# One of 25 products per chunk on another engine, and a new order of loads, in a deformable convolution

## The chip, the cores and the metric

The kernel runs on one core of a Trainium2 chip. The metric is the time on the device in microseconds (us), the median of several runs. A core has five engines with a queue of instructions each: TensorE (PE), VectorE (DVE), ScalarE (ACT), GpSimd (POOL) and SyncE (SP), which here only issues transfers. They run side by side and wait for each other through semaphores. SBUF is the memory on the core, PSUM the banks into which PE accumulates, HBM the memory outside.

## The reference

Four layers follow each other on x of shape (8, 128, 96, 96), each of the form x + f(groupnorm(x)). Layers 1 to 3 (a 3x3 convolution, a depthwise one with signs, a recurrence over rows) are not touched. The change lies in layer 0, a deformable convolution. Cut to what matters:

```python
x1 = gelu(layernorm(depthwise3x3(x)))            # per image
om = x1 @ om_w.T + om_b                          # per pixel and group: 9 offsets (x, y), 9 masks
loc = pixel + tap + offset
samp = bilinear(x, loc)                          # zero outside the image
out = sum over 9 taps of samp * mask
x = x + out
```

There are 8 groups of 16 channels. While every offset is below 1, a bilinear sample is a sum over the 5 x 5 neighbours of a pixel, each with a weight that does not depend on the channel within the group. The kernel uses this: out is the sum of 25 products "weights times shifted rows".

## The kernel before, in words

Layer 0 takes the 8 images one after the other. An image has 12 groups of rows for its depthwise convolution (`NST`), and then 6 **chunks** (`BR`), each made of 16 rows that stand 6 apart; chunk n is chunk n % 6 of image n // 6, 48 in all. The same stage runs for different chunks at the same time:

- **Image** (`image`, once per image, a whole image ahead): SP loads the rows of x into `xq` (L492), DVE takes statistics (L590), ACT normalizes in place (L666), SP writes the normalized rows to HBM as `xnd` (L679, 24 copies per image), PE does the depthwise convolution, nine taps for each group of rows, into the one PSUM bank pair `ps_w` (L720). ACT evicts it to one of two `x1` buffers (L751), SP stores it as `x1d` (L766). In image 0 some groups of rows (`FIRST_ON_DVE`) are convolved on DVE (L710, L712), stored by L770, and the other groups take turns between `ps_w` and `ps_s`.
- **Projection** (`chunk`, some two chunks ahead): SP loads the chunk's rows as `x1c` (L843), ACT applies gelu (L847), PE multiplies by the projection's weights in four pieces, each through `ps_w` (L862), ACT evicts them to `oe` (L870), of which there are two buffers, two pieces in each. SP stores each `oe` to HBM (`omd`, L878) and loads all back in another layout as `om` (L885; one buffer).
- **Tents and weights** (about one chunk ahead): ACT makes from the offsets the three tents `ty` and `tx` per axis (L900 to L909; four buffers of each). POOL multiplies and adds them into the 25 weights per tap position, in three shifts that each begin with L935 (the third one frees `om`), then L941, L950, L958, L960, and two sums L969 into `wx` (two buffers). For chunk 0 two of the three shifts are on DVE.
- **Products**: for each of five vertical shifts, ACT copies the weights into a PSUM bank `ps_wb` (two of them, L1011), and DVE makes five products `pr` = weights x rows (L1023; three `pr` buffers). The rows are in one of five **row slots** `xs` (L827), which hold the chunk's 16 rows at one vertical offset; chunk dy of an image uses slots dy to dy + 4. PE adds each product into `ps_s` through identity matrices (L988: 16 matmuls, which the trace shows as 32 records), after a first addition of the normalized input itself. There is one `ps_s`; ACT evicts it at the chunk's end to `y` (L1055), SP stores `y` (L1072).

In the last chunk seven of the 25 products (`LAST_ON_POOL`) are made by POOL (L1031), straight from `wx`, into an `oe` buffer, since no projection is left that needs it.

The order of every engine's queue is fixed when the program is written out. A planner (`Plan`) gets tasks with an engine, a cost, dependences and a due time; it plays them through and writes each engine's instructions in the order in which it would start them. Due times are multiples of the chunk's length with offsets: `LOAD_AT`, `NORM_AT`, `COPY_AT`, `CONV_AT` for the image's steps, `X1_AT` and `OM_STEP` for the projection, `SLOT_AT` for the row slots, `CONV_BEHIND` for the convolution on PE from image 1 on. Pools marked in order give their buffers in the order in which they were asked for. On the chip the semaphores follow the data only, so a dependence in the planner between tasks that share no data sets nothing but their order.

```python
shared = n == N * BR - 1 and k in LAST_ON_POOL
pr = plan.buf("oe" if shared else "pr")
...
if shared:
    t = plan.task("POOL", 3.65, mul_pool, [*known[sy], slot.load], when - POOL_W, uses=[wx, pr, slot], lag=0.1)
else:
    t = plan.task("DVE", 1.72, mul, [cp, slot.load], when, uses=[wb, pr, slot], lag=0.1)
```

Of the kernel before, what the change touches and what calls it, by code (L numbers as in the profile page):

```python
# [19 lines left out]
P = 128  # L20
# [4 lines left out]
RS = 2  # L25
# [26 lines left out]
    return sorted(every, key=lambda s: (s[0] % NR, s[1] % NR))  # L52


FIRST_ON_DVE = (2, 5, 8, 11)
CH, SHIFT, PE_KEEP = 47.0, 8.6, 4.0
LOAD_AT, NORM_AT, COPY_AT, COPY_LATE, COPY_FROM = -140, -90, -70, 220, 52
CONV_AT, CONV_STEP, CONV_PACE, CONV_GAP = -60, 20, 0.9, 0.0
X1_AT, OM_STEP, SLOT_AT = -95, 2.7, 25
BEHIND, AHEAD, CONV_BEHIND = 40, 60, 40  # L60
HOLD, BEHIND1 = False, 40
LAST_ON_POOL, EACH_ON_POOL, POOL_W = (4, 7, 10, 13, 16, 19, 22), (16,), 20


class Buf:
# [12 lines left out]
class Plan:  # L78
# [20 lines left out]
    def task(self, engine, cost, fn, deps, prio, uses=(), lag=0.05, shape=None, gap=0.0, first=-1e9, move=0.0):  # L99
        t = SimpleNamespace(engine=engine, cost=cost, fn=fn, prio=prio, uses=list(uses), lag=lag, after=[], shape=shape, gap=gap, first=first, move=move)  # L100
        t.number, t.wait = len(self.tasks), len(deps)
        for d in deps:
            d.after.append(t)
        for b in t.uses:
            b.left += 1
        self.tasks.append(t)
        return t
# [94 lines left out]
def kernel(  # L202
# [25 lines left out]
    N, _, H, W = x.shape  # L228
# [7 lines left out]
    NB, HC = 2, P // 2  # L236
    YB, BR = 16, H // 16
# [184 lines left out]
    with ExitStack() as ph:  # L422
# [47 lines left out]
        for name, n, shape, psum, in_order in (  # L470
            ("s", 1, [P, NQ, 512], True, True), ("wb", 2, [P, 512], True, True), ("w", 1, [P, CB, 512], True, False),
            ("xs", 5, [P, GC, XW], False, True), ("pr", 3, [P, GC, W], False, True), ("y", 1, [P, NQ, FB], False, True),
            ("om", 1, [P, 3, K2, W], False, True), ("ty", 4, [P, K2, W], False, True), ("tx", 4, [P, K2, W], False, True),
            ("wx", 2, [P, 3, 3, NS, W], False, True), ("x1", 2, [P, NB, FB], False, False),
            ("x1c", 1, [P, YB, W], False, True), ("oe", 2, [P, YB, W], False, True), 
        ):
            pool = pp if psum else wp
            tiles = [pool.tile(shape, F32, name=f"{'ps_' if psum else ''}{name}{k}") for k in range(n)]
            plan.pool(name, tiles, in_order=in_order)
            if name == "y":  # L480
                spare = tiles[0][:].rearrange("p q f -> p (q f)")[:, : 6 * W].rearrange("p (k w) -> p k w", w=W)
            if name == "wx":
                bias_in, bias_by_g = (tiles[1][0:1, 0, j].rearrange("p s w -> p (s w)")[:, : 3 * GK] for j in range(2))
                put_off(bias_in, om_b.rearrange("k r -> (k r)").unsqueeze(0))

        def load_rows(i, lo, hi, on=nc.sync, js=range(NB)):

            for b in range(NB):
                a, z = (max(lo, RP), hi) if b == 0 else (lo, min(hi, XR - RP))
                top = b * HB - RP  # L490
                for j in js:
                    on.dma_start(xq[half(b), a:z, j, RS : RS + W], x[i, half(j), top + a : top + z, :])  # L492
# [2 lines left out]

            return ap.rearrange("p (b f) -> p b f", b=NB)[:, :, c * FB : (c + 1) * FB]

        free_rows = {}
        smalls = []
        for i in range(2):  # L500
            smalls.append({
# [64 lines left out]
        def image(i, at, before=()):  # L566
# [4 lines left out]
            loads = []  # L571
            step = 1 if i else 2
            for m in range(0, NST, step):
                rows = (0 if m == 0 else RP + m * RB, RP + (m + step) * RB if m < NST - step else XR)
                deps = [t for k in range(m - 1, m + step + 1) for t in free_rows.get((i - 1, k), [])] + list(before)
                when = at + LOAD_AT + 3 * m
                if i:
                    loads += [[task("SP", 2.7, lambda r=rows: load_rows(i, *r), deps, when, lag=0.6, move=1.7)]]
                    continue
                loads += [[  # L580
                    plan.task(e, 2.1, lambda r=rows, on=on, j=j: load_rows(0, *r, on, [j]), [], -1e7 + m, lag=0.6, move=1.7)
                    for j, (e, on) in enumerate((("SP", nc.sync), ("ACT", nc.scalar)))
                ]] * step
            st = small["st"][:].rearrange("p (j m k) -> p j m k", j=NB, k=6)
            stats = []
            for m in range(NST):
                for j in range(NB):
                    stats.append(task(
                        "DVE", 0.55,
                        lambda m=m, j=j: nc.vector.bn_stats(  # L590
                            st[:, j, m, :], xq[:, RP + m * RB : RP + (m + 1) * RB, j, RS : RS + W]
                        ),
                        loads[m][j : j + 1] if i == 0 else loads[m], at + LOAD_AT + 8 + 3 * m,
                    ))
            mv, mean, d, sd, sc, bi = (small[k] for k in ("mv", "mean", "d", "sd", "sc", "bi"))
            mv2 = mv[:].rearrange("p (j k) -> p j k", k=2)
# [16 lines left out]
            def end(ps):  # L613
# [3 lines left out]
            t = plan.task("DVE", 0.9, aggr, stats, -1e6)  # L617
            b1 = plan.buf("w")
            t = plan.task(
                "PE", 0.7, lambda: means(b1.tile), [t, *ready], -1e6, uses=[b1], lag=0.1,  # L620
            )
# [70 lines left out]
            for c in range(NST):  # L692
# [3 lines left out]
                prev = []  # L696
# [32 lines left out]
                for t in range(K2):  # L729
                    if on_dve:  # L730
                        prev = [plan.task(
                            "DVE", 0.92, lambda t=t, tap=tap_dve: [tap(t, j) for j in range(NB)], need + prev,
                            when + CONV_PACE * t, uses=[ps], lag=0.05,
                        )]
                    else:
                        prev = [task(
                            "PE", 0.8, lambda t=t, tap=tap: tap(t), need + prev,
                            when + CONV_PACE * t + (CONV_BEHIND - BEHIND if i else 0), uses=[ps], lag=0.5, shape=32,
                            gap=CONV_GAP if i == 1 else 0.0,
                        )]  # L740
# [78 lines left out]
            slots = {}  # L819
# [15 lines left out]
        def chunk(i, dy, made):  # L835
# [53 lines left out]
                kept, at + X1_AT + 25, uses=[om], lag=0.6, move=4.6,  # L889
            )]  # L890

            wx = plan.buf("wx")
            cols = lambda ap: ap.rearrange("p k w -> p (k w)")
            tent = {}
# [110 lines left out]
            k = 0  # L1005
            for sy in range(NS):
                wb = plan.buf("wb")
                d, y = places[sy]
                cp = plan.task(
                    "ACT", 0.62,  # L1010
                    lambda wb=wb, d=d, y=y: nc.scalar.activation(  # L1011
                        wb.tile[:, : NS * W], wx.tile[:, d, y].rearrange("p x w -> p (x w)"), AF.Identity
                    ),
                    known[sy], at + SHIFT * (sy - 1) - AHEAD, uses=[wb, wx], lag=0.1,
                )
                slot = slots[dy + sy]
                for sx in range(NS):
                    shared = n == N * BR - 1 and k in LAST_ON_POOL
                    pr = plan.buf("oe" if shared else "pr")
                    when = at + SHIFT * sy + SHIFT / NS * sx  # L1020

                    def mul(wb=wb, pr=pr, slot=slot, sx=sx):
                        nc.vector.tensor_tensor(  # L1023
                            pr.tile[:],
                            wb.tile[:, sx * W : (sx + 1) * W].unsqueeze(1).to_broadcast([P, GC, W]),
                            slot.tile[:, :, sx : sx + W],
                            ALU.mult,
                        )

                    def mul_pool(pr=pr, slot=slot, sx=sx, d=d, y=y):  # L1030
                        nc.gpsimd.tensor_tensor(  # L1031
                            pr.tile[:],
                            wx.tile[:, d, y, sx].unsqueeze(1).to_broadcast([P, GC, W]),
                            slot.tile[:, :, sx : sx + W],
                            ALU.mult,
# [6 lines that stand above are left out]
                    k += 1  # L1042
                    adds.append(plan.task(
                        "PE", 0.82,
                        lambda pr=pr, last=(k == NS * NS): add_all(
                            lambda rows32, f: idr[rows32, :],
                            lambda rows32, f: pr.tile[rows32, 4 * f : 4 * f + 4, :],
                            False, last,
                        ),
                        [t, adds[-1]], when + 2, uses=[pr, total], lag=0.5, shape=32,  # L1050
                    ))
# [992 lines left out]
```

## Time and profile before

| | |
|---|---|
| median of 3 runs | 4487.97 us (4481.05 to 4493.4) |
| the profiled execution's own time | 4487.25 us |
| its span, from the first to the last instruction | 4485.5 us |
| of it layer 0 (to the last chunk's end) | about 2440 us |
| mean granted TensorE clock | 0.965 |
| busy over the span: PE, DVE, ACT, POOL | 91%, 87%, 56%, 70% |

A page row of groups reads: line, engine, operation, output <- inputs by the program's names, shapes, count | busy us, mean ns of one | idle time of the engine just before these instructions, and what ended it. A row of waits reads: who waited <- for whom: us in total, times, longest. A row of the stretches reads: stretch, its length, busy us of each engine with the count of its instructions, granted clock, share of the DMA engines, GB/s. A row of the timeline reads: start, length, engine, line, operation, tiles, count. PEld is the weight load of PE.

### The profile page before, as it was taken

The numbers are of one execution on the slowest core, as the hardware profiler recorded it, in microseconds if no ns is written. First come the engines' busy times: TensorE is split into PE (matmuls) and PEld (weight loads), VectorE is DVE, ScalarE is ACT, GpSimd is POOL, SyncE is SP. The second block draws the span as 40 slices with busy tenths as digits, with TensorE's granted clock in tenths as the row PEclk, the third lists the DMA queues.
The fourth block names the chain that finished last, engine by engine and source line by source line (L and its number), as shares of the span: only waits on it lengthen the run. The fifth ranks groups of instructions, "written<-read, shape, count | busy, mean of one in ns | idle before, by whom it ended". The sixth has DMA issues, their size and how long they took to land. (4 is left out here: it accounts for less than half of the span.)

```text
span 4485.5 us, 168975 instructions
## 1 busy us (share of the span) xinstructions
PE 4066.2 (91%) x75910; PEld 2594.3 (58%) x75910; DVE 3915.5 (87%) x4828; ACT 2510.9 (56%) x3579; POOL 3127.5 (70%) x2191
## 2 busy tenths in 40 slices
PE   4598998989989989899866999999999979999999
PEld 2254564545545546455322555555555548999999
DVE  5599999999999999988897589999999967888887
ACT  3545647456475565654542377777887773333332
POOL 0288787877978878788797599999999961222222
PEclk9799999999999999999898999999999989999999
DMA  7765756648566585573632222233222223232231
GB/s 150 192 169 148 207 147 181 183 136 218 146 174 187 138 220 143 158 187 114 178 93 66 62 68 69 72 78 75 69 73 72 63 59 100 88 110 99 99 113 71
DMA packets 756925, 558.03 MB, mean 124 GB/s; under 512 B 616706, under 2 KB 739219, under 8 KB 750051
## 3 DMA queue, kind: packets, MB, share of 16 engines
q1 hardware_dynamic: 723458, 505.33, 41.9%
q10 hardware_dynamic: 32368, 40.25, 2.7%
q8 instruction: 598, 9.80, 0.9%
q0 software_dynamic: 368, 1.57, 0.1%
q14 instruction: 133, 1.08, 0.1%
HBM read 291.39 MB, written 255.66 MB: 122 GB/s over the span
## 5 line engine op out<-in xcount | busy, mean ns | idle before, releaser
L1023 DVE TENSOR_TENSOR pr<-ps_wb,xs 128x1536 f32<-128x1536 f32 x1193 | 2006.4, 1749 | 126.1 <-PE ps_s L988 94.1
L988 PE MATMUL ps_s<-pr,idr 32*32 32x384 f32 x38176 | 1500.9, 507 | 157.5 <-DVE pr L1023 117.6
L988 PEld LDWEIGHTS ps_s<-pr,idr 32*32 32x32 f32 x38176 | 688.3, 104 | 641.9 <-DVE pr L1023 334.2
L720 PE MATMUL ps_w<-xq,dwd 32*32 32x384 f32 x12672 | 901.4, 497 | 33.3 <-issue 23.2
L1520 PE MATMUL pv_C<-dC,km 128*128 128x384 f32 x2304 | 779.6, 492 | 22.8 <-DVE vn L1537 9.7
L1520 PEld LDWEIGHTS pv_C<-dC,km 128*128 128x128 f32 x2304 | 425.7, 190 | 373.4 <-issue 53.4
L1894 POOL TENSOR_TENSOR xtD<-xtD,cr 128x384 f32<-128x384 f32 x192 | 192.5, 1003 | 597.8 <-ACT cr L1893 535.7
L935 POOL TENSOR_TENSOR ty<-ty,om 128x864 f32<-128x864 f32 x142 | 289.3, 2037 | 438.1 <-ACT ty L908 244.4
L1659 DVE SCALAR_TENSOR_TENSOR pd_C<-xqC,w2s,pd_C 128x768 f32<-128x768 f32 x546 | 554.6, 1016 | 41.3 <-ACT pd_C L1687 33.9
L720 PEld LDWEIGHTS ps_w<-xq,dwd 32*32 32x32 f32 x12672 | 400.5, 104 | 217.1 <-issue 115.3
L960 POOL TENSOR_TENSOR wx<-wx,tmp 128x576 f32<-128x576 f32 x284 | 402.8, 1418 | 22.3
L1955 PE MATMUL ps_b<-tr,km 128*128 128x192 f32 x2304 | 407.0, 325 | 0.7 <-DVE tr L1940 0.7
L1955 PE MATMUL ps_a<-tr,km 128*128 128x192 f32 x2304 | 405.4, 324 | 0.0
L958 POOL TENSOR_TENSOR tmp<-tx,ty 128x576 f32<-128x576 f32 x284 | 403.8, 1422 | 0.0
L1676 POOL TENSOR_TENSOR ptC<-ptC,ptC 128x768 f32<-128x768 f32 x222 | 403.0, 1832 | 0.8
L1507 POOL TENSOR_TENSOR dC<-ywC 128x392 f32<-128x392 f32 x384 | 357.3, 958 | 62.6 <-PE pv_C L1520 29.0
L941 POOL TENSOR_TENSOR wx<-tx,ty 128x864 f32<-128x864 f32 x142 | 289.9, 2042 | 145.8 <-ACT tx L907 128.2
L1955 PEld LDWEIGHTS ps_b<-tr,km 128*128 128x128 f32 x2304 | 380.9, 189 | 0.7 <-ACT sd_oC L1795 0.7
L1955 PEld LDWEIGHTS ps_a<-tr,km 128*128 128x128 f32 x2304 | 379.3, 188 | 0.0
L862 PE MATMUL ps_w<-x1c,omg 128*108 128x384 f32 x768 | 321.9, 545 | 47.1 <-ACT x1c L847 24.2
L1011 ACT ACTIVATE ps_wb<-wx 128x480 f32<-128x480 f32 x240 | 136.5, 569 | 407.3 <-DVE pr L1023 367.3
L1667 ACT ACTIVATE ptC<-vn,wsg 128x768 f32<-128x768 f32 x318 | 286.8, 927 | 105.7 <-POOL ptC L1676 53.9
(240 smaller groups left out, 5740.0 us busy)
## 6 DMA issues: line engine op xcount, KB each, us to landing
xs<-xnd SPq DMA_DIRECT2D x80, 800.0 KB
omd<-oe SPq DMA_DIRECT2D x96, 648.0 KB
om<-omd SPq DMA_DIRECT2D x48, 1296.0 KB
xnd<-xq SPq DMA_DIRECT2D x192, 200.0 KB
x1c<-x1d SPq DMA_DIRECT2D x48, 768.0 KB
y<-y SPq DMA_DIRECT2D x192, 192.0 KB
x<-oC SPq DMA_DIRECT2D x192, 192.0 KB
out<-xtD ACTq DMA_DIRECT2D x24, 1536.0 KB
```

Source lines behind the costliest of these rows:

```text
L720: nc.tensor.matmul(ps.tile[to : to + 32, b, :FB], dwd[of : of + 32, j, t, :], xq[of : of + 32, r0 : r0 + RB, j, c0 : c0 + W], start=(t == ...
L862: nc.tensor.matmul(ps.tile[:HM, b, :FB], omg[:, m * HM : (m + 1) * HM], rows[:, f0 : f0 + FB], start=True, stop=True)
L941: lambda on, s: on.tensor_tensor(flat(wx.tile[:, v, :, 1 : NS - 1]), flat(grid(tx)), flat(grid(ty)), ALU.mult),
L958: on.tensor_tensor(part, flat(grid(te)[:, :, ks : ks + 2]), flat(grid(ty)[:, :, ks : ks + 2]), ALU.mult)
L960: on.tensor_tensor(to, to, part, ALU.add)
L988: nc.tensor.matmul(total.tile[32 * f : 32 * f + 32, r, :FB], weights(rows32, f), of(rows32, f), start=first, stop=last)
L1023: nc.vector.tensor_tensor(pr.tile[:], wb.tile[:, sx * W : (sx + 1) * W].unsqueeze(1).to_broadcast([P, GC, W]), slot.tile[:, :, sx : sx + W ...
L1507: lambda k=k, a=a, b=b, op=op: nc.gpsimd.tensor_tensor(d.tile[:, k], yw.tile[:, a : a + CR - 1 : 2, :], yw.tile[:, b : b + CR - 1 : 2, :], op,
L1520: nc.tensor.matmul(flat(ps), km1[:, k, x_, :], d.tile[:, k, :, x_ : x_ + W], start=(x_ == 0), stop=(x_ == 2))
L1659: nc.vector.scalar_tensor_tensor(view, rows8(src, t, h), w[:, t : t + 1], view, ALU.mult, ALU.add)
L1676: lambda a=parts[0], b=pt: nc.gpsimd.tensor_tensor(a.tile[:], a.tile[:], b.tile[:], ALU.add),
L1955: nc.tensor.matmul(ps[:, at_f : at_f + nf], km[:, k, t, :], tr[:, par, :, v : v + HW2], start=(t == 0), stop=(t == NT - 1),)
```

## The change

Three things. From image 1 on (chunk 6), product 10 of each chunk, the first of the third vertical shift, is a task of POOL and takes an `oe` buffer, so that the two `oe` buffers serve the projection and these products; the pool of `oe` no longer gives its buffers in order. In image 0, the loads of all ten row slots are made dependent on the first load of `om`, and the statistics of image 1 on the last tap on DVE; a gate for image 1's row loads is added with a value of 12. And constants change: three groups of rows of image 0 on DVE in place of four, and the due times of loads, normalization, copies, convolution, projection and slots. Lines of the changed kernel stand some 2 to 9 higher: L1023 becomes L1032, L1031 becomes L1040.

```diff
-FIRST_ON_DVE = (2, 5, 8, 11)
+FIRST_ON_DVE = (3, 6, 9)
...
-LOAD_AT, NORM_AT, COPY_AT, COPY_LATE, COPY_FROM = -140, -90, -70, 220, 52
+LOAD_AT, NORM_AT, COPY_AT, COPY_LATE, COPY_FROM = -160, -55, -35, 220, 52
...
-X1_AT, OM_STEP, SLOT_AT = -95, 2.7, 25
-BEHIND, AHEAD, CONV_BEHIND = 40, 60, 40
+X1_AT, OM_STEP, SLOT_AT = -95, 4.0, 50
+BEHIND, AHEAD, CONV_BEHIND = 40, 60, 20
 HOLD, BEHIND1 = False, 40
-LAST_ON_POOL, EACH_ON_POOL, POOL_W = (4, 7, 10, 13, 16, 19, 22), (16,), 20
+GATE, SLOTS_FROM = 12, 0
+LAST_ON_POOL, EACH_ON_POOL, POOL_W = (4, 7, 10, 13, 16, 19, 22), (10,), 20
...
-            ("x1c", 1, [P, YB, W], False, True), ("oe", 2, [P, YB, W], False, True), 
+            ("x1c", 1, [P, YB, W], False, True), ("oe", 2, [P, YB, W], False, False), 
...
                 if i:
+                    deps += first_om if i == 1 and m >= GATE else []
...
-                        loads[m][j : j + 1] if i == 0 else loads[m], at + LOAD_AT + 8 + 3 * m,
+                        loads[m][j : j + 1] if i == 0 else loads[m] + first_dve * (i == 1), at + LOAD_AT + 8 + 3 * m,
...
-                            "DVE", 0.92, lambda t=t, tap=tap_dve: [tap(t, j) for j in range(NB)], need + prev,
+                            "DVE", 1.06, lambda t=t, tap=tap_dve: [tap(t, j) for j in range(NB)], need + prev,
                             when + CONV_PACE * t, uses=[ps], lag=0.05,
                         )]
+                        first_dve[:] = prev
...
+            if n == 0:
+                first_om[:] = moved
+                for j in range(SLOTS_FROM, BR + 2 * RS):
+                    moved[0].after.append(slots[j].load)
+                    slots[j].load.wait += 1
...
-                    shared = n == N * BR - 1 and k in LAST_ON_POOL
+                    shared = k in (LAST_ON_POOL if n == N * BR - 1 else EACH_ON_POOL if n >= BR else ())
```

More of the change, by code (lines that the diff above doesn't have):

```diff
@@ L496, in band_rows @@
             return ap.rearrange("p (b f) -> p b f", b=NB)[:, :, c * FB : (c + 1) * FB]
-        free_rows = {}
+        free_rows, first_dve, first_om = {}, [], []
         smalls = []
```

## The prediction

> **What bounds the kernel now.** I read four views in this order: busy time by stretch, groups of instructions, waits, timeline. The page's chain that ended last is no help here: it follows the last layer back and puts only 6% of the span on VectorE (DVE), while the edit lies in layer 0, the first 2440 us. So I cut layer 0 at the ends of images (columns: stretch, length, then busy us of PE, PEld, DVE, ACT, POOL with counts, clock, DMA).
>
> ```profile
> 766.00:1054.00 288.00, 266.29 (x6836) 153.06 (x6812) 267.43 (x202) 168.00 (x260) 227.34 (x157) 0.96 0.64 170
> ...
> 2192.00:2440.00 248.00, 175.19 (x5041) 61.62 (x5040) 235.92 (x150) 94.42 (x140) 223.62 (x146) 0.94 0.30 89
> ```
>
> Images 1 to 6 (485 to 2192, six such rows) take 1707 us; DVE is busy for 1590 of them, PE 1570, POOL 1354. Two engines at 92 and 93% look like a tie, so the groups and the waits must decide.
>
> ```profile
> L1023 DVE TENSOR_TENSOR pr<-ps_wb,xs 128x1536 f32<-128x1536 f32 x1193 | 2006.4, 1749 | 126.1 <-PE ps_s L988 94.1
> L988 PE MATMUL ps_s<-pr,idr 32*32 32x384 f32 x38176 | 1500.9, 507 | 157.5 <-DVE pr L1023 117.6
> L1031 POOL TENSOR_TENSOR oe<-wx,xs 128x1536 f32<-128x1536 f32 x7 | 22.5, 3233 | 0.1
> ```
> ```profile
> POOL ty L935 <- ACT ty L908: 216.5, 30, 18.8
> PEld ps_s L988 <- DVE pr L1023: 161.1, 233, 4.2
> POOL wx L941 <- ACT tx L907: 100.8, 36, 7.4
> DVE pr L1023 <- PE ps_s L988: 78.3, 73, 3.8
> ```
>
> The second fence is the waits of images 1 to 6. PE's weight loads wait for a product 233 times (161 us), DVE for PE 73 times (78 us), nearly always for a few products at a chunk's boundary, where the sum's single PSUM buffer is evicted. Inside a chunk DVE runs without a gap:
>
> ```profile
> 213.27 26.72 DVE L1023 TENSOR_TENSOR pr<-ps_wb,xs 128x1536 f32<-128x1536 f32 x16
> 2417.49 16.09 POOL L1031 TENSOR_TENSOR oe<-wx,xs 128x1536 f32<-128x1536 f32 x5
> ```
>
> So a product occupies DVE for 26.72/16 = **1.67 us** (1.75 with its tail), POOL for 16.09/5 = **3.22 us**. One addition on PE (32 records) and one convolution tap (16 records, 144 in 6.04 us, so 0.67) together come to about 1.4 us: PE keeps up with a product every 1.67 us and has a little left. DVE sets the pace.
>
> **What the Trainium skill says.** "Perfetto Trace Analysis", section Identifying the Most-Contended Engine: busy share of matmuls is a poor measure of nearness to the limit, that of weight loads a better one. The trace agrees: PE 92%, PEld 153 of 288 us. "GPSIMD Engine Reference", section Engine selection: two-input elementwise work is about twice as slow on GpSimd. Here 3.22 against 1.67, 1.93 times. "SBUF — State Buffer", section Who interferes with whom: a DVE instruction with two SBUF inputs contends with a GpSimd one that reads SBUF, one with at most one SBUF input does not. The trace agrees on both: at 184 us, beside POOL, the SBUF-only L950 took 1.66 to 2.29 us on DVE for two where alone one takes 0.44, while products, whose weights come from PSUM, keep 1748 ns beside a busy POOL. A POOL product hence should not slow the 24 others.
>
> **The change part by part.**
>
> *One product to POOL, chunks 6 to 46 (41 of them; the last chunk keeps its seven).* DVE loses 36 x 1.67 = 60 us in images 1 to 6. PE's work stays. DVE's idle time there is 1707 - 1590 = 117 us, 3.2 per chunk, tied to the boundary, and I expect it to stay or rise a little: I take 93% of 60, **-56 us**; bounds -25 (PE waits take over half) and -75 (the retimed convolution also removes idle time).
>
> POOL gains 3.22 us per chunk on 37.6 busy: 40.8 of a new 45.8. The cover is its idle time, now 9.8 per chunk, which is the two POOL waits above: it waits for tents, which wait for the offsets `om`. I followed this loop chunk by chunk: from POOL's third L935 of a chunk, which frees `om`, to its first of the next takes 11.6 us where nothing is late, exactly the work left in POOL's queue, and 17 on average; it is longest at an image's first chunk (21 to 30: the offsets wait for the image's convolution) and at its third (17 to 23: stores wait behind 24 copies of the next image on SP). In the changed order both shrink: the convolution's last group stands at 4.00 chunks into the image, not 4.42, the first chunk's projection ends 0.08 to 0.15 chunk (4 to 7 us) earlier, and 12 to 16 of the 24 copies now stand before the second chunk's `om` load, which waited anyway. A build also ends with slack: the weights' copy of a chunk's third shift starts 0.4 to 15 us after POOL's last sum, and DVE needs it only one shift (some 8 us) later. The product stands behind that sum, and its addition is the eleventh of the chunk, so 3.22 fits. I take 0 for POOL here.
>
> *Buffer shared with the projection.* The product holds one of two `oe` from about its chunk's start to 0.42 chunk; the projection two chunks on starts at 0.23 with the other and needs a second only after 0.42. In time, 0; if an eviction waits, PE waits behind it (one `w` bank) and DVE after three `pr`: up to 3 us per chunk, 108 in all. The wider step (4.0) is for this spacing.
>
> *Last image.* Here POOL has no cover: 224 busy of 248. From its first L935 of chunk 42 (2161.4) to its last product's end (2433.6) are 272 us. Five products add 16; waits of 2 us at chunks 43 and 46 go (-4); the first chunk's offsets come 7 earlier; the end behind POOL's last product is about 1 shorter than behind DVE's now: **+4**, bounds -8 (DVE's own saving) and +16.
>
> *Start.* Slot loads do not really wait: the dependence is one of the planner's order, so on SP they stand behind the first `om` load. Before, three of them stand between the two `omd` stores:
>
> ```profile
> 143.38 8.18 SPq L827 DMA_DIRECT2D xs<-xnd  x3
> 151.65 0.72 SPq L843 DMA_DIRECT2D x1c<-x1d  x1
> 152.50 6.58 SPq L878 DMA_DIRECT2D omd<-oe  x1
> 166.01 0.32 SPq L885 DMA_DIRECT2D om<-omd  x1
> ```
>
> From the last eviction (147.6) to the `om` issue are 18.4 us; at chunk 12 the same path takes 7.3. So -11. Against it: eight more row loads of image 1 precede the first `x1c` load (0.74 us per issue there, less the moved stores: +4), and the second half of the projection stands between the steps of image 1's coefficients (+2). Together **-5**, bounds -12 and +5. Slots then come after `om`, but the first product needs some 22 us of tents and weights after it, and a load takes some 4.5 us (the third had landed 13.5 us after the first issue, at 141.8), the first needed first.
>
> *Edits costed at nothing.* One of four DVE groups of image 0's convolution goes to PE: DVE saves 9.4 us that it then idles (it waits 16.3 for row loads at 87.5), PE gets 6.0, under evictions that wait for `x1d` stores until 118.8; 0, at worst +6. The gate at 12 is never reached (m ends at 11). Image 1's statistics come after the DVE taps in both orders. Earlier slot loads may spare part of five waits of DVE for `xs` (14.4 us in all).
>
> Sum against the profiled execution, 4487.25 us: -5 - 56 + 4 = -57, so 4430; the median shown is 0.7 higher, and I predict **4430 us**.
>
> **The rivals.** (1) *PE takes the gain.* For: 92% busy, and DVE's 78 us of waits all name it. Against: 161 us of its weight loads wait for DVE. If two thirds of the 56 turn into DVE waits: -5 - 19 + 4, 4467. (2) *POOL becomes the bound: slower.* Place: the loop `om` load, tents, three shifts, product, then the next chunk's first L935. For: it has only 5 us per chunk left, and the last image is its own already. Against: its waits are slack before work that ends early. If the waits shrink by 2.0 instead of 4.8 us per chunk, the cycle grows by 1.2: +44, with the last image's +16 and the start's -5: 4542. It decides from waits above 6.5 us per chunk on; with none removed +117. The shared `oe` would show in the same place. (3) *It does nothing*: the saving goes into other waits wholly, only the start is left: 4482.
>
> **How the numbers follow.** A measurement of this kernel can tell about 0.3%, 13 us. Main case 0.72, between 4403 and 4460 by the bounds of its unknowns; rival 1 0.13, 4455 to 4475; rival 3 0.05; rival 2 0.10, 4500 to 4600. Range 4402 to 4470, which leaves out rivals 2 and 3 and the tails of the rest. Faster by over 0.3%: 0.83; within: 0.06; slower: 0.11.
>
> **What would show it.** Right: L1023 counts 41 fewer, the POOL product 48 at about 3.2 us each; DVE busy about 257 per image of some 274; POOL's waits for ACT fall from 317 to near 180 us in images 1 to 6; the first product near 192 instead of 196.7; the last image near 250. Wrong: DVE's waits for PE over 120 us in images 1 to 6 (rival 1); waits of the weights' copies for POOL, or of L870 for a free `oe`, of more than 1 us per chunk (rival 2); L1023 over 1.8 us beside POOL's product.

## The result, and the profile after

The changed kernel takes 4493.61 us (median of 20 runs) against 4484.04 before: ratio 1.0023, 95% interval 1.0012 to 1.0034, some 10 us slower (5 to 15). The prediction said 4430, in a range of 4402 to 4470. The profiled execution took 4502.73 us, its span is 4500.8 us. Line numbers move with the edit: L988 becomes L997 (PE's additions), L1023 L1032 (DVE's products), L1031 L1040 (GpSimd's), L862 L865 (projection), L870 L873, L878 L881 and L885 L888 (`oe`, `omd`, `om`), L908 and L907 L917 and L916 (tents), L935 and L941 L944 and L950. Of two of the experiments below (e4, the slots freed, and i1, the load times alone) the profiled execution took some 60 to 70 us longer than the median of its kernel; that time lies behind layer 0 (2105 and 2104 us from its end to the last instruction, 2046 before), so of these two traces only layer 0 is read.

The product's rows in the groups of the page after (busy us, mean ns | idle before, releaser):

```profile
L1032 DVE TENSOR_TENSOR pr<-ps_wb,xs 128x1536 f32<-128x1536 f32 x1152 | 1942.0, 1749 | 187.5 <-PE ps_s L997 155.6
L997 PE MATMUL ps_s<-pr,idr 32*32 32x384 f32 x36864 | 1452.2, 507 | 168.0 <-DVE pr L1032 94.3
L1040 POOL TENSOR_TENSOR oe<-wx,xs 128x1536 f32<-128x1536 f32 x48 | 164.9, 3438 | 1.7
```

The 41 products are off DVE, and those that stay take 1749 ns each, as before. But DVE's idle time before L1032 rose from 126.1 to 187.5, and what ended it is PE (94.1 to 155.6). In images 1 to 6 alone, first the stretch (length, busy us of PE, PEld, DVE, ACT, POOL), then the waits:

```profile
500.50:2208.00 1707.50, 1559.76 (x40673) 911.42 (x40673) 1535.83 (x1139) 989.71 (x1521) 1481.87 (x969) 0.97 0.62 169
```
```profile
PEld ps_s L997 <- DVE pr L1032: 145.3, 218, 2.8
...
DVE pr L1032 <- PE ps_s L997: 130.1, 120, 5.8
POOL ty L944 <- ACT ty L917: 128.0, 21, 15.4
...
POOL wx L950 <- ACT tx L916: 66.5, 21, 8.7
```

Before, the same six images took 1707 us with DVE busy for 1590. DVE lost 54 us of work, its waits for PE rose by 52 (78.3 to 130.1), and the time of these images stayed. GpSimd was busy for 128 us more, and its waits for tents fell from 317 to 195 us.

The view that the prediction lacked is the stretches inside one image. Here image 2 of the kernel before, its first four chunks together, then the fifth and the sixth:

```profile
765.70:958.70 193.00, 181.29 (x4711) 108.49 (x4706) 177.51 (x122) 97.50 (x150) 159.41 (x110) 0.97 0.66 171
958.70:1009.90 51.20, 43.22 (x1007) 21.50 (x1008) 47.70 (x57) 31.59 (x49) 37.79 (x26) 0.89 0.54 140
1009.90:1053.90 44.00, 41.99 (x1121) 23.27 (x1121) 42.41 (x26) 39.08 (x67) 30.35 (x21) 0.97 0.63 199
```

Over the image PE and DVE are level (266 and 267 us), but in the first four chunks, where the next image's convolution runs, PE is the busier one. In the fifth, where little of the convolution is left (144 records, 1317 in the four before) and DVE has some of the next image's statistics besides its products, DVE is ahead; in the sixth the two are level. The waits of PE's matmuls in the same execution, first for those four chunks, then for the last two:

```profile
PE ps_s L988 <- DVE pr L1023: 0.6, 1, 0.6
```
```profile
PE ps_s L988 <- DVE pr L1023: 5.8, 8, 1.3
```

In 193 us PE's matmuls waited for a product once, for 0.6 us. The same for all six images, worked out from the traces: chunk ends at the ends of the `y` eviction, means of six; the last column counts only time in which PE neither multiplied nor loaded weights and a product ended it, chunk by chunk. Each row is one execution.

| kernel | length of chunks 1 to 6 of an image, us | PE idle for DVE, us |
|---|---|---|
| before | 50.2, 45.9, 49.8, 44.3, 49.6, 44.7 | 1.0, 0, 0.1, 0, 4.6, 1.9 |
| after | 50.3, 49.5, 47.1, 42.9, 50.6, 44.2 | 0.3, 0, 0, 0.1, 4.8, 1.0 |
| times alone (e2) | 50.3, 50.7, 50.3, 42.0, 53.6, 44.1 | 0, 0, 0.1, 0.1, 7.9, 1.9 |
| order kept, no product (h1) | 51.4, 45.1, 50.2, 44.7, 50.5, 44.4 | 0, 0, 0.1, 0, 4.1, 1.2 |
| order kept, no addition (h2) | 50.6, 45.1, 48.5, 43.4, 50.4, 44.3 | 1.8, 0.1, 0.2, 0.1, 4.4, 2.4 |
| load times alone (i1) | 47.9, 48.3, 46.9, 46.5, 53.0, 45.2 | 0.5, 0.3, 0.3, 0.1, 5.4, 0.8 |
| a tap less (g1) | 44.2, 44.0, 44.7, 42.8, 57.6, 45.4 | 0.7, 0.1, 0, 0.1, 4.6, 1.3 |

So DVE held PE up for about 7.6 us per image, 46 in six, not for the 161 us that PE's weight loads show: a load can wait for a product while the matmuls of earlier ones still run.

These 46 us are a third of the 137 in which PE did nothing in images 1 to 6. Another 51 ended with nothing that the profile shows it to have waited for ("issue"). In the change this part is 94 us; it is 84 to 96 in four executions with all the new times (the change, e2, e4, h4; 70 in e3) and 48 to 71 in twelve with the old ones (35 in i2, 66 and 73 with some of the new, f4 and i1). One of the longest in the change falls into the middle of an addition:

```profile
845.13 1.50 PE L997 MATMUL ps_s<-pr,idr 32*32 32x384 f32 x7 [4.49 <-issue]
```

Nearly all such pauses of over 1 us (23 of 23 before, 34 of 39 in the change) ended 1.1 to 1.8 us after a packet of the DMA queue q8 landed, which the profile calls a queue of instructions; of moments taken at random in these images 13 to 14% do. That points to PE standing still for its own instructions. No experiment here tests it, and what the pauses cost is not known.

### The profile page after: what moved, and what is told of

It is laid out like the page before. It is cut to its first block, busy times and chain, and to the rows that moved or that the text cites. A ratio compares the mean times of both kernels' runs of the same rounds, so it can differ in the third digit from the quotient of the medians.

```text
span 4500.8 us, 169287 instructions
## 1 busy us (share of the span) xinstructions
PE 4071.6 (90%) x76054; PEld 2619.7 (58%) x76054; DVE 3846.0 (85%) x4769; ACT 2511.9 (56%) x3579; POOL 3268.2 (73%) x2232
## 5 line engine op out<-in xcount | busy, mean ns | idle before, releaser
L1032 DVE TENSOR_TENSOR pr<-ps_wb,xs 128x1536 f32<-128x1536 f32 x1152 | 1942.0, 1749 | 187.5 <-PE ps_s L997 155.6
L997 PE MATMUL ps_s<-pr,idr 32*32 32x384 f32 x36864 | 1452.2, 507 | 168.0 <-DVE pr L1032 94.3
L997 PEld LDWEIGHTS ps_s<-pr,idr 32*32 32x32 f32 x36864 | 671.6, 104 | 636.1 <-DVE pr L1032 286.5
L722 PE MATMUL ps_w<-xq,dwd 32*32 32x384 f32 x12816 | 868.2, 494 | 33.9 <-issue 23.9
L944 POOL TENSOR_TENSOR ty<-ty,om 128x864 f32<-128x864 f32 x142 | 289.2, 2036 | 356.8 <-ACT ty L918 178.8
L950 POOL TENSOR_TENSOR wx<-tx,ty 128x864 f32<-128x864 f32 x142 | 289.9, 2041 | 100.3 <-ACT tx L916 84.1
L865 PE MATMUL ps_w<-x1c,omg 128*108 128x384 f32 x768 | 317.7, 539 | 35.7 <-ACT x1c L850 16.2
L1972 ACT ACTIVATE m<-ps_b 128x192 f32<-128x192 f32 x192 | 63.4, 330 | 495.4 <-PE ps_b L1964 495.1
```

Source lines behind the costliest of these rows:

```text
L722: nc.tensor.matmul(ps.tile[to : to + 32, b, :FB], dwd[of : of + 32, j, t, :], xq[of : of + 32, r0 : r0 + RB, j, c0 : c0 + W], start=(t == ...
L865: nc.tensor.matmul(ps.tile[:HM, b, :FB], omg[:, m * HM : (m + 1) * HM], rows[:, f0 : f0 + FB], start=True, stop=True)
L997: nc.tensor.matmul(total.tile[32 * f : 32 * f + 32, r, :FB], weights(rows32, f), of(rows32, f), start=first, stop=last)
L1032: nc.vector.tensor_tensor(pr.tile[:], wb.tile[:, sx * W : (sx + 1) * W].unsqueeze(1).to_broadcast([P, GC, W]), slot.tile[:, :, sx : sx + W ...
```

## The experiments

All ratios are against the kernel before on the same chip, with 95% intervals; 0.1% is 4.5 us. "Product 10" is that of chunks 6 to 46. Expectations speak of the runs made before them.

### The two halves of the change

**e1, the product alone:** before, with

```diff
-shared = n == N * BR - 1 and k in LAST_ON_POOL
+shared = k in (LAST_ON_POOL if n == N * BR - 1 else EACH_ON_POOL if n >= BR else ())
-EACH_ON_POOL = (16,)
+EACH_ON_POOL = (10,)
-("oe", 2, [P, YB, W], False, True)
+("oe", 2, [P, YB, W], False, False)
```

> The kernel before with only the product moved: product 10 of chunks 6 to 46 on GpSimd into a shared oe, every time of the plan (load, normalization, copies, projection step, slots, convolution groups on DVE) as before, no wait of the slots. T1 (GpSimd's own loop, offsets to tents to three shifts to product, is the bound once the product is in it): as after the change or slower, 4485 to 4530, and the lag from GpSimd's third ty of a chunk to its first of the next stays near 17 us. T2 (PE takes the gain: its additions and taps can't follow faster): 4470 to 4490, DVE's waits for PE above 130 us in images 1 to 6. T3 (the retimed plan costs what the product saves): faster than before by 40 to 60, 4425 to 4445.

Measured 1.0038 (1.0022 to 1.0054): 17 us slower. DVE's waits for PE: 151.0 us. The theory that the new times eat a gain of the product (T3) falls. T1 and T2 are not told apart here: the time lies in T1's range and just above T2's; the lag in GpSimd's loop is 17.3 us (17.1 before, 16.9 after the change), as T1 said, and the waits are T2's. Of the 20 us by which the profiled execution is longer than that of before, 7 lie in images 1 to 6 and 9 in the last (257.1 against 248.0), where GpSimd is busy for 244 of 257: the place where the prediction saw no cover for it.

**e2, the times alone:** after, with `EACH_ON_POOL = ()`.

> The changed kernel with all 25 products of chunks 0 to 46 on DVE again: the new times and the slots' wait without the product. T1: slower than before by little, 0 to 20 (image 0 has no product on GpSimd and lost 13 us all the same), images 1 to 6 near 1707 us. T2: the same, 4484 to 4500. T3: slower than before by 50 to 75, 4535 to 4560, with images 1 to 6 near 1765 us.

Measured 1.0083 (1.0065 to 1.0102): 37 us slower. That is in none of the three ranges. So the new plan costs 37 us, and the change, which has the product besides, is 27 faster than that: neither half pays alone.

**e3, the product left out:** after, product 10 planned on no engine.

> The changed kernel, but product 10 of chunks 6 to 46 is made by no engine: PE adds product 9 a second time in its place (the sum so lacks product 10). DVE is relieved as in the change, GpSimd gets nothing and oe is not shared; PE's work is the change's. T1 (GpSimd's 3.2 to 3.4 us, or the shared buffer, is what costs): faster than the changed kernel by 40 to 60, 4430 to 4450. T2 (PE takes the gain): as the changed kernel, 4480 to 4495, DVE's waits for PE above 130 us in images 1 to 6. T3: near the changed kernel too, 4475 to 4495, but then e1 is fast and e2 slow, and under T2 neither is.

Measured 0.9997 (0.9983 to 1.0011), DVE's waits for PE 124.6 us. Taking GpSimd's work and the shared buffer away as well gains 12 us on the change, far from the 40 to 60 of T1; T2 stands nearest, though the waits lie under its 130.

**e4, the slots freed:** after, `SLOTS_FROM = 10`, so that no slot stands behind the first `om` load.

> The changed kernel with the order of the slots' loads behind the first om load undone (all else of the change stays). If that order costs the 13 us of image 0 (its slots come late for chunk 0, or the stores of the projections behind them): image 0 back to 232 us, 4478 to 4484, and the first product as before near 197 us. If the new times cost image 0 its 13 us (stores of the projection held up, om late at chunks 1, 2 and 5): 4490 to 4500, image 0 near 245 us.

Measured 1.0025 (1.0011 to 1.0038), as with the change. The order of the slots costs nothing that this measures.

### Which engine sets the pace

**f1, f2, f3:** before, with product 10 not planned (PE adds product 9 twice), its addition not planned, and neither.

```diff
 # f1
+chosen = k == 10 and BR <= n < N * BR - 1
+if not chosen:
     pr = plan.buf("oe" if shared else "pr")
...
-if shared:
+if chosen:
+    pass
+elif shared:
 # f2, ahead of adds.append
+if k == 11 and BR <= n < N * BR - 1:
+    continue
```

> The kernel before, but product 10 of chunks 6 to 46 is made by no engine; PE adds product 9 a second time instead (product 10 is missing from the sum). DVE loses 41 x 1.67 = 68 us of work, nothing else changes. Theory D (DVE alone sets the pace, the prediction's ground): faster by 60 or more, ratio 0.986 to 0.988. Theory P (PE stands so near behind that it takes most of it; the PE array idles for DVE only 46 us in images 1 to 6 of the trace before): faster by 10 to 35, ratio 0.992 to 0.998, DVE's waits for PE above 120 us in images 1 to 6. Against the product alone (ratio 1.0038 with GpSimd making it) the difference is what GpSimd and the shared buffer cost.

> The kernel before, but PE leaves out its addition of product 10 in chunks 6 to 46 (DVE still makes the product; it is missing from the sum). PE loses 41 additions of about 0.8 us, 33 us. Theory D: no gain, ratio 0.998 to 1.001, since DVE's work is whole. Theory P: part of it is gained, 8 to 25 us, ratio 0.994 to 0.998, DVE's waits for PE fall below 78 us.

> The kernel before with 24 products in chunks 6 to 46: product 10 is neither made nor added (missing from the sum). Theory D: as with the product alone left out, ratio 0.986 to 0.988, because PE never held DVE up. Theory P (two engines with the same pace, so that only both together are worth something): more than the sum of the two single ones, 60 to 80 us, ratio 0.982 to 0.987.

Measured: f1 1.0015 (1.0004 to 1.0025), f2 0.998 (0.9968 to 0.9992), f3 0.9964 (0.9948 to 0.9981). Theory D is dead: 68 us of DVE's work gone, and the kernel is no faster; DVE's waits for PE in images 1 to 6 rose to 139.7 us. But f1 lies above both ranges, f2 on the edge of both, and f3 gained 16 us where P asked for 60 to 80. In f1 the fifth chunk shortened (49.6 to 46.9) and the sixth grew (44.7 to 48.0): leaving a task out of the plan can move the others as well. So the same was done with the order held.

**h1, h2, h3:** before, the tasks stay in the plan and only the instructions are not emitted.

```diff
-t = plan.task("DVE", 1.72, mul, ...
+t = plan.task("DVE", 1.72, (lambda: None) if k == 10 and BR <= n < N * BR - 1 else mul, ...
 # h2 and h3: PE's addition likewise
```

> The kernel before with its planned order held on every engine: the plan still counts product 10 of chunks 6 to 46, but DVE emits nothing there, and PE adds what the buffer held (the sum lacks product 10). So 68 us of DVE work go and no other instruction moves. Theory P (PE sets the pace in the first four chunks of an image, DVE in the last two): only the 14 products of fifth and sixth chunks count, 14 x 1.67 = 23 us at most: faster by 5 to 23, ratio 0.995 to 0.999; chunks one to four unchanged within 1 us each. Theory D (DVE sets the pace): 0.985 to 0.988. Theory O (the earlier 1.0015 with no product was no effect of the order): 1.000 to 1.003.

> The kernel before with its order held, and PE's addition of product 10 of chunks 6 to 46 not emitted (the sum lacks product 10; DVE still makes it). PE loses 41 x 0.83 = 34 us. Theory P: two thirds of it counts, 15 to 27 us, ratio 0.994 to 0.997, all of it in the first four chunks of an image. Theory D: 0.999 to 1.001.

> The kernel before with its order held, product 10 of chunks 6 to 46 neither made nor added (missing from the sum). Theory P: the two single gains add up, 20 to 50 us, ratio 0.989 to 0.9955. Theory D: as with the product alone, 0.985 to 0.988. If a third thing holds the image's period (the run with a tap less gained 38 of 94 us, and taking the product away besides gained nothing more): 0.996 to 0.998 here.

Measured: h1 0.9988 (0.9965 to 1.001), -5 us; h2 0.9963 (0.9949 to 0.9978), -17 us; h3 0.9961 (0.9948 to 0.9974), -17 us. The waits of images 1 to 6 in h1:

```profile
DVE pr L1023 <- PE ps_s L988: 129.9, 126, 4.3
PEld ps_s L988 <- DVE pr L1023: 129.3, 204, 3.4
```

This is the changed kernel's picture (130.1 and 145.3) from nothing but missing DVE work: 78.3 us of waits for PE became 129.9. Counted by the place of the product in its chunk, 30 of these lie at the four products right behind the missing one, where before there were 1.6: DVE has three `pr` buffers, and the time saved turned at once into a wait until PE had added one up. PE's 34 us (0.83 for an addition, the expectation's price) are worth half their length, DVE's 68 at most a quarter (16) and by the median less than a tenth.

Two things that P said did not come true. The gains do not add up: h3 has that of h2 alone, which is its third case, a third thing that holds the image. And in h1 the fifth chunk, where P saw DVE in front, did not shorten (50.5 against 49.6), though DVE worked 1.8 us less in it. That DVE alone sets the pace there is not shown.

**g1, g2, g3:** the ninth of nine taps of PE's convolution left out in images 1 to 7, in the kernel before, in f1 and in e1.

```diff
-for t in range(K2):
+for t in range(K2 - 1 if i else K2):
-    stop=(t == K2 - 1),
+    stop=(t == (K2 - 2 if i else K2 - 1)),
```

> The kernel before, but the convolution on PE of images 1 to 7 leaves out its ninth tap (the convolution so lacks one of nine taps). PE loses about 13.5 us per image, some 94 in all, four fifths of it in the first four chunks of each image. Theory P (in those chunks PE sets the pace: it waited for DVE 1.1 us per image there, in chunks five and six 6.5 us): they shorten until DVE binds, which idles 14.9 us per image there; faster by 50 to 80, ratio 0.982 to 0.989, DVE's waits for PE in images 1 to 6 well under 78 us. Theory L (a loop outside both, offsets to tents to GpSimd, or ACT, sets the pace): ratio 0.994 or above.

> The kernel before with the ninth tap left out as in the run with a tap less, and product 10 of chunks 6 to 46 made by no engine (PE adds product 9 twice). Theory P: with room on PE, DVE's 68 us are worth something at last: faster than a tap less alone by 25 to 55, ratio 0.970 to 0.981; without that room they were worth nothing (1.0015). Theory L: no more than with a tap less alone.

> The kernel before with the ninth tap left out, and product 10 of chunks 6 to 46 on GpSimd in a shared oe (the change's product with the plan of before). Theory P: faster than a tap less alone by 15 to 45, GpSimd and the shared buffer taking back the 10 us that they took back before; ratio 0.973 to 0.984. If GpSimd's loop becomes the bound once chunks get shorter: as a tap less alone or slower.

Measured: g1 0.9914 (0.9885 to 0.9942), g2 0.9909 (0.988 to 0.9939), g3 0.9913 (0.9886 to 0.994). The expectation overpriced the tap: by a burst of nine (6.04 us) it is 0.67 us, 0.67 x 12 x 7 = 56 us in all (PE's busy time in images 1 to 6 fell by 49). 39 us were gained, below P's 50 to 80, but 70% of the work, where P's figures were 53 to 85% of its 94. The place is P's: the first four chunks fell from 190.2 to 175.7 us per image. They were rid of 5.9 us of DVE's work as well as of 10.0 of PE's, however, so the fall is not PE's alone. The fifth gave 8 back (49.6 to 57.6). Image 2 of g1, the same three stretches:

```profile
771.10:944.30 173.20, 168.61 (x4575) 96.58 (x4574) 169.60 (x112) 93.03 (x146) 145.36 (x100) 1.00 0.65 178
944.30:1003.50 59.20, 43.42 (x972) 19.61 (x964) 55.56 (x67) 34.29 (x51) 44.20 (x31) 0.90 0.56 153
1003.50:1047.20 43.70, 41.73 (x1104) 22.69 (x1104) 40.31 (x25) 39.99 (x69) 37.96 (x26) 0.95 0.71 202
```

More of the statistics now fall into the fifth chunk (14 of its instructions per image, 8 before), where DVE works for 55.56 of 59.20. Yet the product, left out or moved, brought nothing more, where P expected 15 to 55 us: g2 shortens that chunk to 50.1 and lengthens the four before it to 180.6. These two are plans made anew, like f1. What then holds the image near 277 us (275 to 279 in the three) was not found.

### What the rest of the change costs

**f4:** the times alone (e2), with `OM_STEP` 2.7 and `CONV_BEHIND` 40 as before.

> The changed kernel's plan without the product on GpSimd (the run of the times alone: ratio 1.0083), with the two constants that move PE's work put back: projection step 2.7 and convolution 40 behind. If these two are what costs 37 us (they move the taps and projections among the additions, and PE is the engine with no room): ratio back to 0.999 to 1.003. If the others (loads, normalization, copies, slots, three groups on DVE instead of four) do: ratio stays at 1.006 to 1.010.

Measured 1.0056 (1.0035 to 1.0077), just under the second range: 25 of the 37 us stay.

**i1:** before, with only

```diff
-LOAD_AT, NORM_AT, COPY_AT = -140, -90, -70
+LOAD_AT, NORM_AT, COPY_AT = -160, -55, -35
-SLOT_AT = 25
+SLOT_AT = 50
```

> The kernel before with four of the change's times alone: row loads 20 earlier, normalization and copies 35 later, slots 25 earlier. In the traces so far image 0 took 226 to 240 us (mean 234) with the times of before and 238 to 245 (mean 242) with those of the change, whether or not the product, the slots' wait or the projection's step was in. If these times are the cause: image 0 near 241 us and ratio 1.002 to 1.008. If the third convolution group on DVE less (three instead of four) and the order of image 1's statistics behind it are: image 0 near 234, ratio 0.998 to 1.002.

Measured 1.0064 (1.0042 to 1.0087): four due times, and not one instruction more or less, cost 29 us. In the trace of i1 images 1 to 6 are 21 us longer than before, and 20 of them lie in the fifth chunk (53.0 us against 49.6, table above). In e2, which has these times too, that chunk is as long (53.6). Image 2 of e2:

```profile
984.60:1039.60 55.00, 42.76 (x1033) 19.34 (x1016) 51.57 (x60) 42.47 (x67) 37.91 (x26) 0.91 0.50 142
```

Here the fifth chunk is 55.0 us instead of 51.2, DVE is busy for 51.57 of it, 60 instructions instead of 57, and ACT for 42.47 instead of 31.59. ACT's part is the next image's normalization: before it fell whole into the sixth chunk, in e2 three quarters of it, on the mean of six images, fall into the fifth. The statistics have not moved (8 instructions there before and in e2). But normalization cannot be what the 29 us rest on: in i1 only a quarter of it lies there and ACT is busy for 32.3 us on the mean of six, hardly more than before (30.7). The place is shown, why the chunk grows there is not. In the change it is shorter again:

```profile
976.30:1027.40 51.10, 43.69 (x1032) 20.19 (x1016) 48.76 (x57) 42.09 (x66) 48.98 (x33) 0.87 0.51 142
```

Over six images the fifth chunk is 3.0 us shorter than in e2 (50.6 against 53.6), 18 us of the 38 by which images 1 to 6 differ in these two executions (e2's was 4533.02 us, 19 above its median; the change's 9 above). The rest was not traced.

**h4:** after, GpSimd's product of chunks 6 to 46 not emitted, the order held.

> The changed kernel with its planned order held, but GpSimd emits no product in chunks 6 to 46; PE adds what the shared buffer held (the sum lacks product 10). Rows 96 to 127 of the two oe buffers are cleared once at the start. GpSimd is relieved of 41 x 3.4 = 141 us and PE's addition waits for nothing; everything else is the change. If GpSimd's product costs what the run with it left out from the plan showed (12 us, ratio 0.9997 of before): 0.998 to 1.001. If all of that was the order: as the changed kernel, 1.001 to 1.004. If GpSimd's loop is the bound of the changed kernel: 0.990 or below.

Measured 1.0026 (1.0006 to 1.0045), the changed kernel's 1.0023 again. GpSimd's 141 us, its place in the offsets' loop and PE's wait for it cost nothing that this measures in the plan of the change; the 12 us of e3 therefore were mostly the planner's new order, though the two intervals (0.9983 to 1.0011 in e3) overlap a little. With the plan of before (e1) this was not tried.

### Two tries at something faster

**g4:** before, products 10 and 18 on GpSimd only in each image's fifth chunk (`n % BR == 4`).

> The kernel before with products moved to GpSimd only where PE waits for DVE: products 10 and 18 of the fifth chunk of images 1 to 7, in a shared oe; every other product stays on DVE. DVE loses 7 x 2 x 1.67 = 23 us. Theory P: these chunks (49.6 us on average, PE idle for DVE 4.6) shorten by 2 to 3 us each: faster by 8 to 20, ratio 0.9955 to 0.998, unless the next chunk gives it back as it did with no product made (fifth chunk -2.7, sixth +3.3): then 0.999 to 1.002. Theory L: 1.000 to 1.003.

Measured 1.0029 (1.0013 to 1.0044). The fifth chunk shortened by 0.9 us where 2 to 3 were expected, the second grew by 2.2; a miss.

**i2:** e1, and one of the twelve convolution groups of images 1 to 7 on DVE (`c in (FIRST_ON_DVE if i == 0 else (5,))`).

> The product alone on GpSimd with the plan of before (ratio 1.0038), and in images 1 to 7 one of the twelve convolution groups on DVE instead of PE: DVE gets 9.4 us per image back of the 10.0 that the products took off it, PE loses 6.0 per image, 42 in all. With half to two thirds of PE's relief counting, as in the runs with an addition or a tap less: 20 to 28 us faster than the product alone, ratio 0.997 to 0.9995. If the group's 9.4 us on DVE, which hold one of three product buffers, starve PE at that place, or the new order costs as much: 1.001 or above.

Measured 1.0159 (1.0102 to 1.0216), 71 us slower. First and second chunk of image 2:

```profile
778.60:824.70 46.10, 44.79 (x1191) 24.59 (x1177) 40.52 (x30) 22.93 (x37) 40.24 (x27) 1.00 0.87 219
824.70:886.30 61.60, 50.40 (x1151) 27.62 (x1144) 60.44 (x43) 30.16 (x50) 47.26 (x29) 0.89 0.53 150
```

The second chunk takes 61.6 us with DVE busy for 60.44. PE is idle for products there for 10.1 us per image, a place that had none. The group's nine taps (two instructions each) alternate with single products, and some take far longer than others:

```profile
824.83 4.65 DVE L712 SCALAR_TENSOR_TENSOR pr<-xq,dwq,pr 128x384 f32<-128x384 f32 x2
829.40 1.74 DVE L1023 TENSOR_TENSOR pr<-ps_wb,xs 128x1536 f32<-128x1536 f32 x1
831.06 1.13 DVE L712 SCALAR_TENSOR_TENSOR pr<-xq,dwq,pr 128x384 f32<-128x384 f32 x2
```
```profile
825.41 3.64 POOL L1031 TENSOR_TENSOR oe<-wx,xs 128x1536 f32<-128x1536 f32 x1
```

The slow pair runs beside GpSimd's product. In images 1 to 6 such a tap, which reads SBUF alone, took 0.60 to 0.61 us where GpSimd was idle, 1.75 beside L960 and 3.8 beside L1031, and the group 14.6 to 22.4 us per image, 20 on the mean, not the expected 9.4. So DVE did not get back what the products took off it, but about twice that, while one of three `pr` was held. Whether an even sum would have helped was thereby not tested. No version with the whole work beat the kernel before.

## Why the prediction was wrong, step by step

- **"DVE sets the pace", 93% of 60 us, -56: the step that failed.** Its sizes were right (DVE's busy time fell by 54), its worth was not: about -5 (-16 to +4) for all 68 us with the order held (h1), 7% instead of 93%, outside the bound of -25 too. Instead the saving went into DVE's waits for PE, 78.3 to 129.9 us in h1. Five readings led there. The tie of 93 and 92% was judged over whole images, where it hides four chunks in which PE hardly lacks a product (1.1 us per image) and two in which it does (6.5). The 161 us of weight loads waiting for DVE were held against rival 1 as room on PE, while PE stood still for DVE for 46 us only; the row of waits that would have said so (PE for DVE, 43.4 us) was passed over. The share of weight loads, which the prediction preferred to that of matmuls, pointed the same wrong way: 53% of an image, and yet h2 shows PE's work to be worth half its length. And the gapless 26.72 us of DVE were taken for any chunk's inside; they lie in chunk 0, and PE was busy for 23.43 of them as well. The 1.4 us of PE per product left out the projection, four pieces of 1.54 us per chunk in the trace before, by estimate a quarter of a microsecond per product, which is nearly all of the room up to 1.67.
- **GpSimd at 0: right.** Its waits for ACT fell to 195 us (predicted near 180), the product took 3.44 us instead of 3.22, and h4 shows no cost. The lag of its loop did not shrink as the prediction thought (17.1 to 16.9 us); the product simply filled its waits. Rival 2 did not happen.
- **Shared `oe` at 0: right.** PE waited for a product of GpSimd once in images 1 to 6, for 1.1 us.
- **Last image +4 (-8 to +16): right within its bounds**, 248.0 to 246.9, but not by its reasons alone: with the times of before (e1) it is +9, and e2, with the new times and no product, has 246.9 too.
- **Start -5: wrong by 8.** Chunk 0 ended at 255.5 instead of 252.5. From the last projection's eviction to the `om` issue are 7.4 us, as predicted (7.3), but that eviction came at 160.4 instead of 147.7: gelu started 4.9 later (+4 was predicted), and the second half of the projection between the coefficients of image 1 took 7.9 more (+2 was predicted). 2.7 of these are PE's clock: the granted clock was 0.50 there (1.00 before), and each of the last two pieces took 2.9 us instead of 1.54. The first product came at 200.2, not near 192. PE's queue after:

```profile
143.70 2.90 PE L865 MATMUL ps_w<-x1c,omg 128*108 128x384 f32 x4 [0.99 <-ACT oe L873]
...
150.04 2.90 PE L865 MATMUL ps_w<-x1c,omg 128*108 128x384 f32 x4 [1.55 <-DVE d L330]
...
156.64 2.87 PE L865 MATMUL ps_w<-x1c,omg 128*108 128x384 f32 x4 [2.13 <-DVE bi L337]
```

- **Edits costed at nothing: wrong.** The plan without the product costs 37 us (e2), and four due times alone, put into the kernel before, 29 (i1). The sign is not theirs only: with the old times the product made the kernel slower too (e1, 17 us). Image 0, which has no product on GpSimd, took 241.6 us from the end of its first chunk to that of its last on average in five kernels with the new times (238 to 245; after, e2, e3, f4, h4) and 232.3 in nine with the old (226 to 238; before, e1, f1 to f3, g4, h1 to h3). That is 9 us; i1, with four of the times, has 238.7, and which of them does it was not separated. The prediction named these edits one by one and asked of each whether its work was covered, not whether the chunk that it went into had room.
- **Rival 1 named the right place**: DVE's waits for PE over 120 us were its sign, and they came out at 130. It was priced at two thirds of the gain, where nearly all of it went; and no rival carried the new times as a cost. The bounds of the prediction's own terms add up to 4392 to 4483, wider than the 4403 to 4460 that it gave its main case, and the result lies above even these.

Put together: +37 for the plan, -27 from there to the change, +10. The second figure is only the difference of the other two, no check of them.

## What to carry to other kernels

Where two engines are level over a whole period, cut the period at its phases, and count for each engine only the time in which it stands still for the other: the weight loads' waits (161 us here, against 46 of standstill) can say little about room. Where PE hardly ever waited for a product, 68 us less of DVE's work became waits for a free buffer. Due times can cost more than such a move could bring (29 us in i1), with no instruction added. When a planner writes the order, an experiment that leaves a task out tests the new order too; keep the task in the plan and leave out the instruction.

## What the runs showed of the hardware

A product on GpSimd beside 24 on DVE did not slow these: 1749 ns with 41 more of them on GpSimd, as before. GpSimd's own took 3.43 to 3.50 us in chunks 6 to 46; of the seven in the last chunk before, four took 3.46 to 3.49 and three 2.91 to 2.92, so that their mean of 3.23 is the time of none.

DVE's taps, which read SBUF alone, fared otherwise beside GpSimd: 0.60 to 0.61 us where it was idle, up to 3.8 beside its product (i2).

The granted clock of TensorE fell in the same phase in these four plans, the fifth chunk of image 2: 0.89 before, 0.87 after, 0.91 in e2, 0.90 in g1, where the four chunks before it had 0.97 to 1.00. That is the chunk with the least of the convolution. What triggers it, and what it adds to that chunk's length, was not tested.
